# Two attention blocks: k and q by a seven-product scheme applied twice, partial sums moved between PSUM banks

## The chip, the cores and the metric

The kernel runs on one core of a Trainium2 chip. The metric is the device time of one execution, in microseconds (us). A core has TensorE (PE, matmul; PEld is its weight load), VectorE (DVE), ScalarE (ACT), GpSimd (POOL) and a sync engine (SP) whose queue issues the DMAs. Each engine works through its own instructions in the order in which the program lists them, and waits on semaphores for the others. Matmul results land in PSUM, which has eight banks of 512 fp32 columns on each of 128 partitions.

## The reference

Two attention blocks follow each other, each with its own weights; the second has the same form under other names. The input has 8 images of 512 channels and 32x32 = 1024 positions, all in fp32.

```python
xn = group_norm(x, 8 groups) * gamma + beta
qkv = einsum('oc,bchw->bohw', qkv_w, xn) + qkv_b          # 512 -> 3 * 512
q, k, v = split into 8 heads of 64
attn = softmax(einsum('bhds,bhdt->bhst', q, k) * 64 ** -0.5)
out = einsum('bhst,bhdt->bhds', attn, v)
x = x + einsum('oc,bchw->bohw', proj_w, out) + proj_b
```

## The kernel before

There are 16 jobs, one for each image and layer: images 0 and 1 in layer 0, then both in layer 1, then images 2 and 3, and so on. A job `n` has four 512x512 by 512x1024 products (k, q, v and the output projection, here K, Q, V, O) and the attention.

**The four products.** Each is cut into 2x2 blocks, and a scheme with seven block products in place of eight is applied once. The block of the weights goes through seven factors (`A11, A12, A22, S1..S4`; four of them are sums that VectorE makes once, in `factor`), and the other operand through sums in `tx` (for `xn`) or `to` (for the attention's output), made by `combine`. `product` issues one of the seven for one half `i` of the rows: two matmuls of 128x128 by 512 columns (L277), or for V four of 256 columns (L270). In the trace each fp32 matmul appears as two MATMUL records with a weight load each. `seven` runs the seven products for one `i`, in the order 1, 2, 6, 5, 7, 3, 4. It holds four PSUM banks `z, y, u, v`. Products 1, 6 and 7 add up in bank z, and after each of them `note` copies the partial sum out to SBUF before the next product adds to it; `join` adds what lies in SBUF to a bank and writes the result.

**The order of a job.** The loop over `n` is, for neighbouring jobs: attention of `n`, then K of `n+1`, O of `n`, V of `n+1`, Q of `n+1`, then attention of `n+1`. In Q's second half, `first_scores` puts the first two steps of the attention between the products.

**The attention.** It has 64 steps (four head pairs, two halves of the queries, eight key blocks of 128). A step is `scores` (four matmul groups on 64x64 quadrants, L470, into two PSUM banks `sc`), ScalarE's exp into a tile of `epool` (L475), VectorE's running sum `acc` (L479, L481), and `values` two steps later (L495). `epool` has four tiles; a tile is free once all its readers are done. `finish` closes each group of eight steps.

**What sets the order.** TensorE, ScalarE and VectorE keep the order of the program text. A small planner spreads side work: `later(delay, fn)` lists a function for a time on the planner's own clock, and `advance(us)`, called after each product and step, moves that clock and runs what is due. `chores` are side work tied to a step of the attention: the statistics (`reads`) and the normalisation (`steps`) of the next job. Tiles with the same tag share buffers: a tile's first write waits for the last reader of the one before. DMAs go out on SP's queue in order. `fetch` loads one whole weight matrix with all seven factors (1792 KB) into `wpool`, where each of K, V, Q, O has one buffer; on first use it loads the four raw blocks, and the finished factors are kept in DRAM (`keep`).

## Time and profile before

| What | Value |
|---|---|
| median of 4 runs | 3362.03 us (3360.58 to 3362.49) |
| the profiled execution | 3360.58 us; its span 3358.8 us |
| instructions | 50799 |
| TensorE busy | 3327.2 us (99% of the span) |
| VectorE busy | 2320.0 us (69%) |
| ScalarE busy | 1379.9 us (41%) |
| chain that ended last, by line | L470 27%, L495 25%, the products of L277 and L270 45% |
| granted TensorE clock | 0.999 |

How to read it: the span is one execution under the hardware profiler. The chain that ended last is followed back from the last instruction, at each step to what released it. A row of a group gives line, engine, operation, output<-inputs, shapes and count; behind the bar the busy time and the mean duration in ns of one; behind the second bar the engine's idle time just before these instructions and what ended it. In a timeline row the first number is the start and the second the duration. Matmuls are pipelined and their ends are modelled, so that neighbouring MATMUL rows overlap; the distance of their starts is what counts.

### The profile page before, as it was taken

How to read it: one execution, taken by the hardware profiler on the slowest of the kernel's cores; microseconds unless marked ns; L12 is line 12 of the kernel's file. 1: busy time of each engine (PE TensorE's matmuls, PEld its weight loads, DVE VectorE, ACT ScalarE, POOL GpSimd, SP SyncE). 2: the span in 40 equal slices, each digit the busy share in tenths (PEclk: the TensorE clock that was granted, in tenths of full speed). 3: DMA queues.
4: the chain of work that ended last, by engine and by line, in shares of the span. 5: the costliest groups of instructions: out<-in, count | busy, mean ns of one | idle time of the engine just before them, and what ended most of it. 6: DMA issues, size and time to landing. Idle time of an engine off the chain costs nothing.

```text
span 3358.8 us, 50799 instructions
## 1 busy us (share of the span) xinstructions
PE 3327.2 (99%) x20996; PEld 1481.8 (44%) x20996; DVE 2320.0 (69%) x3192; ACT 1379.9 (41%) x1535; POOL 16.9 (1%) x26
## 2 busy tenths in 40 slices
PE   7999999999999999999999999999999999999999
PEld 4335353453534535344353443535435354353533
DVE  4775957759487584865839668486684966848566
ACT  1543615336163361633516245162451624526153
POOL 0000000000000000000000000000000000000000
PEclk9999999999999999999999999999999999999999
DMA  5011010120201100021010010002102001000101
GB/s 194 12 51 51 22 60 15 53 81 22 76 15 36 48 24 23 15 74 63 22 72 18 33 52 21 23 18 83 52 21 73 18 33 52 21 22 22 45 11 44
DMA packets 79535, 141.82 MB, mean 42 GB/s; under 512 B 37568, under 2 KB 45760, under 8 KB 75200
## 3 DMA queue, kind: packets, MB, share of 16 engines
q1 hardware_dynamic: 79296, 138.50, 11.9%
q8 instruction: 166, 2.72, 0.3%
q14 instruction: 73, 0.60, 0.1%
HBM read 104.35 MB, written 31.98 MB: 41 GB/s over the span
## 4 chain that ended last, share of the span: by engine, by line
PE 98%; ACT 1%; DVE 0%; issue 0%; DMA 0%; POOL 0%; SPq 0%; DVEq 0%; POOLq 0%
PE sc L470 27%; PE po L495 25%; PE z L277 15%; PE u L277 10%; PE z L270 5%; PE y L277 5%; PE v L277 5%; PE u L270 3%; PE y L270 2%; PE v L270 2%; ACT e L475 1%; PE pp L440 1%; DVE stats L189 0%; DMA x<-x_dram 0%; ACT xn L225 0%
## 5 line engine op out<-in xcount | busy, mean ns | idle before, releaser
L475 ACT ACTIVATE e<-sc 128x1024 f32<-128x1024 f32 x1024 | 1047.0, 1024 | 645.4 <-PE sc L470 564.7
L470 PE MATMUL sc<-q,k 64*64 64x512 f32 x8192 | 1063.4, 591 | 6.6 <-ACT e L475 6.6
L495 PE MATMUL po<-e,v 64*64 64x512 f32 x8192 | 1057.3, 589 | 0.0
L481 DVE TENSOR_TENSOR acc<-acc,e 128x1024 f32<-128x1024 f32 x768 | 937.4, 1221 | 101.2 <-ACT e L475 52.9
L495 PEld LDWEIGHTS po<-e,v 64*64 64x64 f32 x8192 | 313.3, 133 | 565.6 <-issue 556.5
L470 PEld LDWEIGHTS sc<-q,k 64*64 64x64 f32 x8192 | 307.1, 133 | 565.1 <-issue 543.5
L326 ACT ACTIVATE sa<-z,vec_sb 128x512 f32<-128x512 f32 x128 | 88.0, 688 | 446.1 <-PE z L277 440.3
L277 PE MATMUL z<-xn,w 128*128 128x512 f32 x512 | 244.0, 599 | 3.6 <-ACT xn L225 3.6
L479 DVE TENSOR_TENSOR acc<-e,e 128x1024 f32<-128x1024 f32 x128 | 156.5, 1222 | 116.8 <-ACT e L475 115.5
L406 ACT ACTIVATE sb<-z,vec_sb 128x512 f32<-128x512 f32 x30 | 20.6, 688 | 340.9 <-PE z L277 340.9
L507 DVE TRANSPOSE_TENSOR_REDUCE r<-acc 128x32 f32<-128x1024 f32 x128 | 158.6, 1239 | 0.6
L378 ACT COPY sb<-u 128x512 f32<-128x512 f32 x32 | 18.8, 586 | 337.5 <-PE u L270 337.5
L277 PEld LDWEIGHTS z<-xn,w 128*128 128x128 f32 x512 | 96.4, 191 | 124.5 <-issue 119.1
L277 PE MATMUL z<-t,w 128*128 128x512 f32 x256 | 121.9, 599 | 4.7 <-DVE w L155 4.7
L277 PE MATMUL u<-xn,w 128*128 128x512 f32 x256 | 122.0, 599 | 0.0
L270 PE MATMUL z<-w,xn 128*128 128x256 f32 x512 | 121.0, 379 | 0.0
L277 PE MATMUL u<-t,w 128*128 128x512 f32 x256 | 120.5, 593 | 0.0
L277 PE MATMUL y<-xn,w 128*128 128x512 f32 x256 | 120.3, 592 | 0.0
L277 PE MATMUL v<-t,w 128*128 128x512 f32 x256 | 120.3, 592 | 0.0
L330 DVE TENSOR_TENSOR q<-sb 128x512 f32<-128x512 f32 x32 | 22.2, 693 | 137.9 <-ACT sb L326 137.9
L537 DVE TENSOR_TENSOR q<-q,rb 128x512 f32<-128x512 f32 x128 | 86.6, 677 | 40.4 <-DMA rb<-rd 40.4
L277 PE MATMUL z<-q,w 128*128 128x512 f32 x240 | 112.8, 592 | 0.0
(106 smaller groups left out, 2695.7 us busy)
## 6 DMA issues: line engine op xcount, KB each, us to landing
w<-keep SPq DMA_DIRECT2D x24, 1792.0 KB, 7.2
rb<-rd SPq DMA_DIRECT2D x256, 128.0 KB, 2.9
x<-x_dram SPq DMA_DIRECT2D x32, 512.0 KB, 5.5
out_dram<-x SPq DMA_DIRECT2D x64, 256.0 KB, 2.0
keep<-w SPq DMA_DIRECT2D x8, 1792.0 KB, 5.7
lr<-r SPq DMA_DIRECT2D x512, 4.0 KB, 1.7
w<-wqkv_dram SPq DMA_DIRECT2D x24, 256.0 KB, 5.1
w<-wp_dram SPq DMA_DIRECT2D x8, 256.0 KB, 6.1
```

The lines of the kernel that those rows point to most:

```text
L270: nc.tensor.matmul(ps[:, ti * CH : (ti + 1) * CH], block[:, cc, t0 : t0 + P], w[:, slot, cc, :], start=(first and ti == 0 and cc == 0), st ...
L277: nc.tensor.matmul(ps, w[:, slot, cc, i * P : (i + 1) * P], block[:, cc, :], start=(first and cc == 0), stop=(cc == 1), skip_group_check=True,
L326: nc.scalar.activation(out, ps, AF.Identity, bias=env.vec(layer, bias, oc))
L330: nc.vector.tensor_add(dst[:, 2 * oh + i, cols], a, b)
L440: nc.tensor.matmul(ps, w[:, cc, oc * P : (oc + 1) * P], qt[0][:, cc, cols], start=(cc == 0), stop=(cc == NC - 1),)
L470: nc.tensor.matmul(sc[h * HD : (h + 1) * HD, j, :], k[r, hp, k0 : k0 + HD], q[r, hp, sh * HALF : (sh + 1) * HALF], start=True, stop=True,)
L475: nc.scalar.activation(e, sc, AF.Exp, scale=SCALE)
L479: nc.vector.tensor_add(acc[g], es[i - 1], e)
L481: nc.vector.tensor_add(acc[g], acc[g], e)
L495: nc.tensor.matmul(po[g][j * HD : (j + 1) * HD, h, :], v[r, kc, d0 : d0 + HD], e[r, j, :], start=(kc == 0), stop=(kc == NT - 1),)
L507: nc.vector.tensor_reduce(r, a.rearrange("p j (b e) -> p (j b) e", e=RP), AX.X, ALU.add, apply_transpose=True,)
L537: nc.vector.tensor_mul(q[:, hp, cols], q[:, hp, cols], rb)
```

## The change

K and Q use the scheme twice: each of the seven outer block products is itself cut into 2x2 blocks, so that 49 products of 128x128 by 256 columns replace 28 matmuls of 512 columns. `deep_phases` builds 14 chains (seven outer products for K, seven for Q). A chain runs the seven inner products with four banks. Chains alternate on the two halves of PSUM and overlap: chain c's inner product j has slot 7c + 2j, so that in the steady state neighbouring slots belong to two chains. The result of an outer product (a tile of `epool`) is added into its quarter of k or q by `end`, on VectorE. The inner sums of the moving operand are made by `deep_sums` in the stages before.

In all four products a partial sum no longer goes to SBUF: in `chain`, ScalarE copies bank z to y after product 1 and to u after product 6, and the next product adds onto the copy. The bias of v moves into the output bias, made once per layer by `make_out_bias` with 16 one-column matmuls. `bias` in `deep_phases` gives outer products 2, 3, 4 and 5 a bias, and 1, 6 and 7 none. At the start eight matmuls write all banks once.

Weights stream through `ring`, eight tiles that hold one factor each (V, O) or the seven inner factors of one outer factor (K, Q). The inner factors are made in `prepare` at first use and kept in DRAM. The first layer's factors of V, K and Q are made at the start, the others as chores of the attentions of jobs 0 to 2 (`first_factors`). The order of a job becomes: attention of `n`, V of `n+1`, O of `n`, K and Q of `n+1`. The `to` sums take the tag k instead of v. `load_blocks` and `store_factors` are the DMAs of the former `fetch`, taken apart. V and O interleave their two halves.

The diff, cut to its core (the functions that it removes are printed above):

```diff
+FACTOR = {1: A11, 2: A12, 3: S4, 4: A22, 5: S1, 6: S2, 7: S3}
+ORDER = (1, 5, 6, 2, 7, 3, 4)
+OUTER = (1, 2, 6, 5, 7, 3, 4)
+QT = HALF // 2
+RING = 8
...
-    wpool = ctx.enter_context(tc.tile_pool(name="wpool", bufs=1))
+    ring = ctx.enter_context(tc.tile_pool(name="ring", bufs=RING))
...
+    plan, held, raw = deque(), {}, set()
+    def fetch():
+        if not plan:
+            return
+        key = plan.popleft()
+        n, which, o = key
+        layer = jobs[n][1]
+        w = ring.tile([P, NW, P], F32, tag="w", name=f"w_{which}_{n}_{o}")
+        held[key] = w
+        src = factors[which, layer][:, FACTOR[o]]
+        if which in (V, O):
+            nc.sync.dma_start(wide(w), src)
+        elif (which, layer, o) in deep:
+            nc.sync.dma_start(w, deep[which, layer, o])
+        else:
+            for at, i, j in ((A11, 0, 0), (A12, 0, 1), (A22, 1, 1), (S3, 1, 0)):
+                nc.sync.dma_start(w[:, at], src[:, j, i * P : (i + 1) * P])
+            raw.add(key)
+    def prepare(key):
+        if key not in raw:
+            return
+        raw.discard(key)
+        n, which, o = key
+        w = held[key]
+        for part in range(4):
+            factor(w, part)
+        keep = wdram.tile([P, NW, P], F32, name=f"deep_{which}_{jobs[n][1]}_{o}")
+        deep[which, jobs[n][1], o] = keep
+        later(1.0, lambda: nc.sync.dma_start(keep, w))
+    def used(key):
+        del held[key]
+        later(2.5, fetch)
...
+    def chain(product, put5, put, z, y, u, w):
+        def step(o):
+            product(o, {1: z, 5: w, 6: z, 2: y, 7: z, 3: u, 4: z}[o], o in (1, 5))
+            if o == 1:
+                nc.scalar.copy(y, z)
+            elif o == 5:
+                put5(w)
+            elif o == 6:
+                nc.scalar.copy(u, z)
+            elif o == 2:
+                put(0, 0, y)
+            elif o == 7:
+                put(1, 1, z)
+            elif o == 3:
+                put(0, 1, u)
+            else:
+                put(1, 0, z)
+        return step
+    def half_phase(n, which, src, t, group, order):
+        steps = []
+        for i in range(2):
+            z, y, u, w = (bank(i, b, f"{b}_{which}_{n}_{i}") for b in "zyuv")
+            steps.append(chain(*group(i), z, y, u, w))
+        thunks = []
+        for o in order:
+            key = (n, which, o)
+            thunks.append(lambda o=o: (steps[0](o), advance(1.72)))
+            def second(o=o, key=key):
+                steps[1](o)
+                if key in held:
+                    used(key)
+                advance(1.72)
+            thunks.append(second)
+        return thunks
...
+            def put(oh, sh, ps):
+                t0 = sh * NT // 2 + 2 * i
+                to_ = dst[:, t0 : t0 + 2, oh * CH : (oh + 1) * CH]
+                if sh == 0:
+                    nc.scalar.copy(to_, tokens(ps))
+                else:
+                    nc.vector.tensor_add(to_, tokens(ps), tokens(s5))
...
+            def put5(ps):
+                for oh in range(2):
+                    nc.vector.tensor_add(s5[:, oh, :], ps, at(oh, 1))
+            def put(oh, sh, ps):
+                oc = 2 * oh + i
+                more = s5[:, oh, :] if sh == 1 else at(oh, 0)
+                nc.vector.scalar_tensor_tensor(
+                    at(oh, sh), ps, out_bias[:, layer, oc : oc + 1], more, ALU.add, ALU.add
 +                )
...
+        chains = [(K, o) for o in OUTER] + [(Q, o) for o in OUTER]
+        tiles = {}
+        def begin(c):
+            which, o = chains[c]
+            if o == OUTER[0]:
+                name = "k" if which == K else "q"
+                dst[which] = acts.tile([P, NC, S], F32, tag=name, name=f"{name}_{n}")
+            if c + 2 < len(chains):
+                prepare((n,) + chains[c + 2])
+            e = epool.tile([P, 2, HALF], F32, tag="e", name=f"p_{n}_{c}")
+            tiles[which, o] = e
...
+            half = c % 2
+            z, y, u, w = (
+                bank(half, b, f"{b}d_{n}_{c}")[:, :QT] for b in ("vyuz", "zyuv")[(c // 2) % 2]
+            )
...
+            def put(oo, ph, ps):
+                to_ = e[:, oo, ph * QT : (ph + 1) * QT]
+                b = bias(oo)
+                if ph == 0:
+                    if b is None:
+                        nc.scalar.copy(to_, ps)
+                    else:
+                        nc.scalar.activation(to_, ps, AF.Identity, bias=b)
+                elif b is None:
+                    nc.vector.tensor_add(to_, ps, s5)
+                else:
+                    nc.vector.scalar_tensor_tensor(to_, ps, b, s5, ALU.add, ALU.add)
+            return chain(product, lambda ps: nc.scalar.copy(s5, ps), put, z, y, u, w)
+        def end(c):
+            which, o = chains[c]
+            used((n, which, o))
+            d = dst[which]
+            def quarter(oh, sh):
+                return d[:, 2 * oh : 2 * oh + 2, sh * HALF : (sh + 1) * HALF]
+            def p(k):
+                return tiles[which, k]
+            if o == 2:
+                nc.vector.tensor_add(quarter(0, 0), p(1), p(2))
+            elif o == 6:
+                nc.vector.tensor_add(p(6), p(6), p(1))
+            elif o == 5:
+                nc.vector.tensor_add(quarter(0, 1), p(6), p(5))
+            elif o == 7:
+                nc.vector.tensor_add(p(7), p(7), p(6))
+                nc.vector.tensor_add(quarter(1, 1), p(7), p(5))
+            elif o == 3:
+                nc.vector.tensor_add(quarter(0, 1), quarter(0, 1), p(3))
+            elif o == 4:
+                nc.vector.tensor_add(quarter(1, 0), p(7), p(4))
+        live = {}
+        def thunk(c, j):
+            def go():
+                if j == 0:
+                    live[c] = begin(c)
+                live[c](ORDER[j])
+                if j == 6:
+                    end(c)
+                advance(0.43)
+            return go
+        at = sorted((7 * c + 2 * j, c, j) for c in range(len(chains)) for j in range(7))
+        return [thunk(c, j) for _, c, j in at]
...
+            to[0] = acts.tile([P, 3, 2, HALF], F32, tag="k", name=f"to_{n}")
             combine(src, to[0], 0)
...
+    def deep_sums(n, direct_at, other_at):
+        def start():
+            d = acts.tile([P, 4, 7, QT], F32, tag="deep", name=f"deep_{n}")
+            deep_x[0], deep_t[0] = d[:, :, :4, :], d[:, :, 4:, :]
+        later(direct_at - 0.1, start)
+        for part in range(4):
+            later(direct_at + 1.7 * part, lambda part=part: inner_sums(part, True))
+            later(other_at + 1.7 * part, lambda part=part: inner_sums(part, False))
...
+    def first_blocks(w, layer, which, delay):
+        for part in range(4):
+            later(delay + 1.7 * part, lambda part=part: factor(w, part))
+        later(delay + 6.0, lambda: store_factors(w, layer, which))
+    def make_out_bias(w, layer):
+        pb = two_banks("sc", f"pb_{layer}")
+        for oc in range(NC):
+            for cc in range(NC):
...
+                nc.tensor.matmul(
+                    pb[:, 0, oc : oc + 1], w[:, at, cc % 2, o0 : o0 + P],
+                    env.vec(layer, BV, cc), start=(cc == 0), stop=(cc == NC - 1),
+                )
...
+    first = v_phase(0, (1, 2, 6, 5, 7, 3, 4), v0)
+    for thunk in first[:4]:
+        thunk()
+    for step in (
+        t[0], t[1], lambda: factor(v0, 0), lambda: factor(v0, 1), t[2], lambda: factor(v0, 2),
+        lambda: factor(v0, 3), t[3],
+    ):
+        step()
+    store_factors(v0, 0, V)
+    first_blocks(k0, 0, K, 0.1)
+    deep_sums(0, 7.0, 14.0)
+    def second_blocks():
+        q0 = acts.tile([P, NW, 2, CH], F32, tag="k", name="raw_q0")
+        load_blocks(q0, 0, Q)
+        first_blocks(q0, 0, Q, 6.0)
+    def first_plan():
+        plan.extend((0, K, o) for o in OUTER)
+        for _ in range(len(OUTER)):
+            fetch()
+    def second_plan():
+        plan.extend((0, Q, o) for o in OUTER)
+        fetch()
+    later(7.5, first_plan)
+    later(9.0, second_blocks)
+    for thunk in first[4:-1]:
+        thunk()
+    advance(0.0)
+    rest = first[-1:]
+    for n in range(-1, len(jobs)):
...
+                if n == 0:
+                    first_factors(more, [(O, 0), (V, 1)])
+                elif n == 1:
+                    first_factors(more, [(K, 1), (Q, 1)])
+                elif n == 2:
+                    first_factors(more, [(O, 1)])
...
+                chores[61] = lambda: (extend_plan(n + 1), [fetch() for _ in range(RING)])
...
+            out_sums(n, qt[0])
+            deep_sums(n + 1, 4.0, 27.0)
+            for thunk in v_phase(n + 1, ORDER):
+                thunk()
+            proj = proj_phase(n)
+            for thunk in proj[:-1]:
+                thunk()
+            rest = proj[-1:]
+        both = deep_phases(n + 1)
+        prepare((n + 1, K, OUTER[0]))
+        prepare((n + 1, K, OUTER[1]))
+        both[0]()
+        rest[0]()
+        if n >= 0 and jobs[n][1] == 1 and jobs[n][0] + 2 < B:
+            load_x(jobs[n][0] + 2)
         reads = steps = []
+        if n + 2 < len(jobs):
             reads, steps = norm_steps(n + 2)
+            if jobs[n + 2][1] == 1:
+                for i, step in enumerate(reads):
+                    later(9.0 + 6.0 * i, step)
+                reads = []
+        for i, thunk in enumerate(both[1:-3]):
+            if n < 0 and i == 14:
+                second_plan()
+            thunk()
+        att_n = n + 1
+        banks(0, "two")
+        att = Attention(att_n)
+        att.scores(0)
+        both[-3]()
+        att.scores(1)
+        both[-2]()
+        both[-1]()
+        banks(1, "two")
```

## The prediction

> **What bounds the kernel now.** The page comes first: busy shares, then the chain that ended last.

> ```profile
> PE 3327.2 (99%) x20996; PEld 1481.8 (44%) x20996; DVE 2320.0 (69%) x3192; ACT 1379.9 (41%) x1535; POOL 16.9 (1%) x26
> PE 98%; ACT 1%; DVE 0%; issue 0%; DMA 0%; POOL 0%; SPq 0%; DVEq 0%; POOLq 0%
> ```

> TensorE ends every stage, so a product removed there is time removed, as long as nothing new makes TensorE wait. Next the windows, for two stages of one job: K with O and V with Q are alike, here V, then the attention.

> ```profile
> 256.80:281.00 24.20, 24.20 (x113) 21.30 (x113) 9.69 (x15) 1.17 (x2) 0.00 (x0) 1.00 0.00 1
> 305.20:416.40 111.20, 110.76 (x1022) 39.49 (x1020) 95.81 (x126) 70.54 (x73) 1.01 (x1) 1.00 0.09 26
> ```

> The columns are length, then busy time of PE, PEld, DVE, ACT. VectorE has room in a projection stage and little in the attention. Third the timeline, for the price of a product and of handing over.

> ```profile
> 28.96 0.69 DVE L155 TENSOR_TENSOR w<-w 128x512 f32<-128x512 f32 x1
> 29.77 0.30 PEld L277 LDWEIGHTS z<-t,w 128*128 128x128 f32 x2 [5.46 <-issue]
> 38.44 1.88 PE L277 MATMUL v<-t,w 128*128 128x512 f32 x4
> ...
> 40.15 1.88 PE L277 MATMUL z<-t,w 128*128 128x512 f32 x4
> 40.35 0.69 DVE L330 TENSOR_TENSOR k<-v,sb 128x512 f32<-128x512 f32 x1 [0.82 <-PE v L277]
> ...
> 47.02 1.88 PE L277 MATMUL v<-t,w 128*128 128x512 f32 x4
> ...
> 55.64 1.89 PE L270 MATMUL z<-w,xn 128*128 128x256 f32 x8
> ...
> 62.55 1.89 PE L270 MATMUL y<-w,xn 128*128 128x256 f32 x8
> ```

> Five products of 512 columns lie between 38.44 and 47.02: 1.716 us each. Four of 256 columns, twice as many matmuls, lie between 55.64 and 62.55: 1.728. A reader starts 0.20 after the next product starts (40.15, 40.35); TensorE restarts 0.12 after VectorE ends (29.65, 29.77). Fourth the groups by shape:

> ```profile
> L326 ACT ACTIVATE sa<-z,vec_sb 128x512 f32<-128x512 f32 x128 | 88.0, 688 | 446.1 <-PE z L277 440.3 <-DVE k L330 4.5 <-DVE acc L481 1.3
> L323 ACT COPY sb<-u 128x512 f32<-128x512 f32 x64 | 37.5, 586 | 67.4 <-PE u L277 58.8 <-DVE q L330 7.5 <-DVE w L159 1.1
> L248 DVE TENSOR_TENSOR t<-xn 128x1024 f32<-128x1024 f32 x16 | 19.5, 1219 | 0.0
> L153 DVE TENSOR_TENSOR w<-w 128x512 f32<-128x512 f32 x8 | 5.5, 684 | 1.7 <-DMA w<-wqkv_dram 1.7
> L270 PEld LDWEIGHTS u<-w,t 128*128 128x128 f32 x256 | 48.6, 190 | 6.6
> ```

> **Columns.** K and Q are now 28 products of 1.716 = 48.05 a job; then 98 products of a quarter of 1.728, 0.432 = 42.34. Saved: 5.7 a job. [...]

> **The loop of a chain.** Two chains alternate on TensorE, one product each. Call them A and B, B seven products behind. Product 4 of B adds onto bank z, so VectorE's put after B's product 7 must have read z before. Ahead of this put in VectorE's queue stands end, the quarter add of A, and that waits for ScalarE's copy-out after A's product 4. So from A's product 4 to B's, seven products or 3.02 us later, this must fit:
> - the product 0.43 and the handover 0.20;
> - the copy-out 0.47 (688 for 512 columns, less 256 at 0.83 ns, the slope between the 512 columns of L323 and the 1024 of L475, 1024 ns), and 0.03 to VectorE;
> - the add 1.14 (1.22, less the 0.08 by which neighbours overlap: 29.57 starts before 29.65 in the timeline);
> - the put 0.48 (L408's 751 less 256 at VectorE's 1.04 ns) and 0.12 back to TensorE.

> That is 2.87, and 3.06 with a weight load of 0.19 that can't run ahead of the wait. It just closes, since both long forms (with bias) meet only once in seven. I take no loss; the bounds are 0 and 0.3 a chain. After outer product 7, end makes two adds, the second dependent on the first: 1.25 more with no room for it. TensorE's queue is in order, so I take 1.2 of waiting, once in K and once in Q: +2.4 a job, bounds 2.0 and 2.7. The other new waits are short. Product 6 needs ScalarE's copy from z to y: it has three products, 1.29 us, for 0.20 + 0.37 + 0.06 + 0.19. In V and O a slot is 1.72 us, so the same waits have four times the room; their VectorE work falls (V makes 4 puts for 14 notes and joins). [...]

> **Entry to attention.** Step 2's exp needs a tile of epool. Of its four tiles two hold exps 0 and 1, and two hold outer products 7 and 4 until the last end. Count from the end of the last product: exp 1 ends at 0.36 (it follows scores 1, two products earlier), then VectorE works off the first acc add, a put and the last end: 0.36 + 1.22 + 0.43 + 1.14 = 3.15. Exp 2 runs from 3.2 to 4.2 instead of from 1.15. Scores 4 need its bank; scores 2 and 3 and values 0 and 1 before them last 4 x 0.86 + 0.1 = 3.5. So scores 4 start at 4.3: +0.8 a job, bounds 0 and 1.2.

> **Other steps in steady state.** bn_stats for a layer-1 job (two of 0.67 and one of 0.21) come inside K and Q, in eight jobs, four each; the loop leaves VectorE 1.0 free per 3.02, so each overhangs 0.3: +9 in all, bounds 0 and 16. Inner sums (8 adds) lie in V and O, whose VectorE time falls. Jobs 0 and 2 prepare weights: four adds of 128x128 at 0.28 (684 less 384 columns), 1.0 ahead of a put with 0.15 spare: 0.85 for some eight chains, +7 for job 2, bounds 4 and 10. make_out_bias: 16 matmuls of one column, 32 weight loads at 0.19, plus restart: 7, twice, +14, bounds 8 and 22. Ring fetches are eight tiles ahead; one issue of about 0.5 on SP per 3 us; behind them queue only the sums' small DMAs: nothing. The factor adds in attention 0 to 2 (5 us in 111) fit.

> **The start.** Its DMA prices:

> ```profile
> 232.78 1.95 SPq L147 DMA_DIRECT2D w<-wqkv_dram  x4
> ...
> keep<-w SPq DMA_DIRECT2D x8, 1792.0 KB, 5.7
> w<-wqkv_dram SPq DMA_DIRECT2D x24, 256.0 KB, 5.1
> ```

> Four V products end at 25.0, as K's do now; the 4.7 us gap behind them closes, since VectorE makes no joins before the sums. V ends at 25.0 + 10 x 1.73 = 42.3. VectorE, with no joins to wait for, has V's factors at 24.5 and K's four at 28.5. Both are stored, 5.7 each: K's lie in DRAM about 36. first_plan then puts 28 small loads (seven tiles of four blocks) on SP, which wait for that store: 28 at 0.49 (1.95 for four) end at 50. Q's four blocks are queued behind them: issued to 52, landed at 57. By the planner's clock their factors come 16 us after V's fourth product, which is at the end of V, so they stand in VectorE's queue ahead of the put of the first chain. VectorE waits to 57 and works 4 us off (two factors of 0.68, two inner sums of 0.9, one preparation of 1.0). TensorE comes to product 4 of that chain nine products after V, at 46, and goes on at 61. K's first quarter add also waits for Q's blocks to be stored (same tag k): +3.5. Restart at half clock +1.6, preparation +7, double adds +2.4, 89 products 38.4, two scores 1.7: scores 2 at 115.6, against 99.1 in the trace: +17, bounds 6 and 26.

> **Sum.** 15 jobs x (-5.7+2.4) = -50; entry 16x0.8 = +13; statistics +9; job 2 +7; out_bias +14; start +17: **+10**. The profiled execution took 3360.6 with a span of 3358.8, 1.4 under the median 3362.0; on the median this is 3372. The half widths (start 10, out_bias 7, statistics 8, entry 8, double adds 5, preparation 3) combine to about 18: its own range is 3354 to 3390.

> **Rivals.** (1) The double adds are absorbed: a wait shifts later work, so the loop could regain it, and VectorE has 1 us free a turn. Against it: the products behind the waiting one are held in order. It decides where 0.9 of each 1.2 is regained in the 30 waits (-27: 3345, faster by 0.5%); with all of it -36: 3336. With the entry free too, 3323. (2) The loop doesn't close: copy from bank to bank, which no row shows, or the weight load costs 0.3 more than 3.02 allows, in each chain: 224x0.3 = +67, 3439; it decides from 0.05 a chain (+11). (3) The products are bound by weight loads: two of 0.190 in 0.432 leave 0.05; if waits keep loads from running ahead, 98x0.05x16 = +78, 3450.

> **How the numbers follow.** Forecast 0.48, rival 1 0.27, rival 2 0.18, rival 3 0.07. Within 0.2% (6.7 us), about what a measurement can tell from no change: the forecast gives 0.09 faster, 0.21 same, 0.70 slower; rival 1 gives 0.85, 0.10, 0.05; the others are slower. Sum: faster 0.27, same 0.13, slower 0.60. The range, 3334 to 3415, holds the forecast, most of rival 1 and the weaker half of rival 2.

> **What would show it.** TensorE waiting on VectorE's put once per K and once per Q, about 1.2 us; eight products of 256 columns still 3.46 us; scores of job 0 beginning about 17 us later, behind a VectorE wait for Q's blocks; scores 4 of each job waiting for exp. If TensorE shows waits at every chain, rival 2 is right; if K and Q last 42.4 us, rival 1; a job under 203 us from attention to attention (207.9 now; the forecast makes it 205.4) would break the forecast.

## The result, and the profile after

The changed kernel took 3366.2 us (median of 40 runs, 3361.9 to 3370.0) where the kernel before took 3361.9 (60 runs): ratio 1.0013, interval 1.0008 to 1.0017. It is slower by 4.3 us. The prediction was 3372, with 3334 to 3415 as its range and "slower" as its likeliest case.

The profiled execution has a span of 3363.0, 4.2 above that of before, and took 3364.9. The page's busy shares and its chain that ended last, after:

```profile
PE 3283.5 (98%) x22420; PEld 1740.9 (52%) x22420; DVE 2602.9 (77%) x3630; ACT 1727.4 (51%) x2557; POOL 17.5 (1%) x30
PE 90%; DVE 6%; ACT 2%; DMA 1%; issue 1%; SPq 0%; POOL 0%; DVEq 0%; ACTq 0%
```

TensorE is busy 43.7 us less and the span is longer all the same: TensorE's share of the chain went from 98% to 90%, and VectorE's from 0 to 6%. One job's attention and then the four projections behind it, as two windows (length, then busy time of PE, PEld, DVE, ACT):

```profile
953.86:1064.05 110.19, 109.16 (x1017) 38.67 (x1016) 101.92 (x138) 70.92 (x75) 1.01 (x1) 1.00 0.07 19
1064.05:1160.55 96.50, 94.47 (x385) 68.92 (x381) 63.66 (x93) 37.09 (x86) 0.00 (x0) 1.00 0.36 108
```

TensorE, which had next to no gap before, now stands idle about 1 us in the attention and 2 in the projections. The view of waits, TensorE's own, says for whom (total, times, longest):

```profile
PE vd L486 <- DVE p L502: 30.7, 32, 2.2
PE sc L593 <- ACT e L598: 16.0, 46, 0.6
PE vd L486 <- DVE p L500: 15.1, 5, 12.7
```

The first line is 32 waits for a put, two a job; the second is the entry to attention; the third is mostly one wait of 12.7, at the start.

The timeline of one double add (start, length; TensorE, ScalarE and VectorE lines about it, others left out):

```profile
1129.91 1.03 PE L486 MATMUL vd<-deep,w 128*128 128x256 f32 x4
...
1130.16 1.17 DVE L524 TENSOR_TENSOR p<-p,p 128x1024 f32<-128x1024 f32 x1
...
1131.37 1.23 DVE L525 TENSOR_TENSOR k<-p,p 128x1024 f32<-128x1024 f32 x1
...
1132.51 0.48 DVE L502 SCALAR_TENSOR_TENSOR p<-vd,bias_step,s 128x256 f32<-128x256 f32 x1
...
1133.05 0.70 PE L486 MATMUL vd<-deep,w 128*128 128x256 f32 x2 [1.25 <-DVE p L502]
```

Both adds of `end` (L524, L525) run ahead of the next chain's put (L502), and product 4 of that chain waits 1.25 for it. (K and Q of this job also read statistics for the next one; a reading ends at 1130.25, just ahead of the adds.) The last line lasts 0.70, against 0.59 elsewhere: its weight load starts with it at 1133.05, where that of the row behind, at 1133.58, starts 0.21 ahead. Counted from start to start of the products, TensorE loses 1.51 here and 1.05 in a job without statistics.

The timeline of the entry to attention, at the start of the period whose end holds these adds:

```profile
955.72 1.23 DVE L529 TENSOR_TENSOR q<-p,p 128x1024 f32<-128x1024 f32 x1
956.48 1.04 PE L618 MATMUL po<-e,v 64*64 64x512 f32 x8
957.03 1.94 ACT L598 ACTIVATE e<-sc 128x1024 f32<-128x1024 f32 x2 [2.60 <-DVE q L529]
...
958.11 1.09 PE L593 MATMUL sc<-q,k 64*64 64x512 f32 x8 [0.59 <-ACT e L598]
```

Exp 2 waits 2.60 for the last quarter add (L529) to free a tile, and scores 4 wait 0.59 for that exp. The other 30 waits of that line, 0.2 each at steps 25 and 33, are in the kernel before as well.

### The profile page after: what moved, and what is told of

It reads as the page before. It is cut to its first block, busy times and chain, and to the rows that moved or that the text cites. A ratio compares the mean times of both kernels' runs of the same rounds, so it can differ in the third digit from the quotient of the medians.

```text
span 3363.0 us, 56688 instructions
## 1 busy us (share of the span) xinstructions
PE 3283.5 (98%) x22420; PEld 1740.9 (52%) x22420; DVE 2602.9 (77%) x3630; ACT 1727.4 (51%) x2557; POOL 17.5 (1%) x30
## 3 DMA queue, kind: packets, MB, share of 16 engines
q1 hardware_dynamic: 154176, 259.12, 24.3%
## 4 chain that ended last, share of the span: by engine, by line
PE 90%; DVE 6%; ACT 2%; DMA 1%; issue 1%; SPq 0%; POOL 0%; DVEq 0%; ACTq 0%
PE sc L593 26%; PE po L618 25%; PE vd L486 6%; PE z L384 6%; PE z L419 6%; PE zd L486 6%; PE yd L486 2%; PE ud L486 2%; ACT e L598 2%; PE u L384 2%; PE v L384 2%; PE y L384 2%; PE u L419 2%; PE y L419 2%; PE v L419 2%; DVE p L524 1%
## 5 line engine op out<-in xcount | busy, mean ns | idle before, releaser
L486 PE MATMUL vd<-deep,w 128*128 128x256 f32 x960 | 278.5, 388 | 45.8 <-DVE p L502 30.7
L486 PE MATMUL zd<-deep,w 128*128 128x256 f32 x832 | 235.9, 383 | 5.4 <-DVE p L502 2.8
L486 PEld LDWEIGHTS vd<-deep,w 128*128 128x128 f32 x960 | 178.6, 191 | 98.5 <-DVE p L502 43.5
L486 PEld LDWEIGHTS zd<-deep,w 128*128 128x128 f32 x832 | 156.6, 191 | 41.7 <-DVE p L502 7.5
L335 ACT COPY yd<-vd 128x256 f32<-128x256 f32 x128 | 45.7, 357 | 185.5 <-PE vd L486 178.2
L426 DVE TENSOR_TENSOR s5o<-v,x 128x512 f32<-128x512 f32 x60 | 38.6, 684 | 101.9 <-PE v L419 101.9
L419 PE MATMUL z<-to,w 128*128 128x512 f32 x240 | 110.3, 592 | 0.0
L384 PE MATMUL z<-w,t 128*128 128x256 f32 x480 | 108.5, 379 | 0.0
L384 PEld LDWEIGHTS z<-w,xn 128*128 128x128 f32 x480 | 90.0, 190 | 23.8 <-issue 12.2
L384 PEld LDWEIGHTS z<-w,t 128*128 128x128 f32 x480 | 91.2, 190 | 12.4
## 6 DMA issues: line engine op xcount, KB each, us to landing
w<-keep SPq DMA_DIRECT2D x210, 256.0 KB, 2.7
out_dram<-x SPq DMA_DIRECT2D x64, 256.0 KB, 3.4
keep<-raw SPq DMA_DIRECT2D x5, 1792.0 KB, 5.8
```

Source lines behind the costliest of these rows:

```text
L335: nc.scalar.copy(y, z)
L384: nc.tensor.matmul(ps[:, ti * CH : (ti + 1) * CH], r[:, cc, t0 : t0 + P], w[:, cc, :], start=(start and ti == 0 and cc == 0), stop=(cc == ...
L419: nc.tensor.matmul(ps, w[:, cc, i * P : (i + 1) * P], r[:, cc, :], start=(start and cc == 0), stop=(cc == 1), skip_group_check=True,)
L426: nc.vector.tensor_add(s5[:, oh, :], ps, at(oh, 1))
L486: nc.tensor.matmul(ps, lhs[:, FACTOR[i], :], moving[i], start=start, stop=True, skip_group_check=True,)
```

## Where the time went, step by step

In the trace, one number carries each job: the time from its scores 2 to the next job's scores 2. Before it is 207.89 in fourteen of the fifteen periods and 208.00 in one. After, the twelve periods from job 3 on take 205.41 (six, without statistics) and 206.6 (six, with). Each period holds the attention and O of one job and V, K and Q of the next, so each term of the prediction's sum has a place of its own:

| stretch | prediction, us against before | measured |
|---|---|---|
| start, to scores 2 of job 0 | +17 (115.6) | +13.5 (112.6) |
| job 0 to 1: out_bias, statistics | +5.6 | +2.6 |
| job 1 to 2: preparation, statistics | +5.6 | +6.6 |
| job 2 to 3: out_bias | +4.5 | +3.0 |
| six periods without statistics | 6 x -2.5 | 6 x -2.48 |
| six with statistics | 6 x -1.4 | 6 x -1.27 |
| last attention | +0.8 | +1.1 |
| sum | +10 | +4.2 |

The steady state was forecast to 0.1 us a job. The difference of 6 us lies in the start and the three early periods (7.0 below the forecast, against 1.2 above it in the rest), and the runs below say why.

## Experiments

Every ratio is to the kernel before, run on the same chip (its median there lay between 3361.7 and 3362.6); "the changed kernel" is the 3366.2 above. Periods and starts are read from one profiled execution a run; "attention 0 begins" stands for the start of scores 2 of job 0 in it.

**1. The second add later.** After outer product 7, `end` writes its quarter in one add and leaves the other for a later thunk:

```diff
-                nc.vector.tensor_add(p(7), p(7), p(6))
-                nc.vector.tensor_add(quarter(1, 1), p(7), p(5))
+                nc.vector.tensor_add(quarter(1, 1), p(7), quarter(0, 1))
+                held_back.append(lambda: nc.vector.tensor_add(p(7), p(7), p(6)))
...
+                if j == 5 and held_back:
+                    held_back.pop()()
```

> After outer product 7, end makes one add (quarter(1,1) = p(7) + quarter(0,1)); the second, p(7) += p(6), is issued behind the two puts of the next chain. The sum and the number of adds stay the same. Theory (VectorE's queue order: two dependent adds of 1.22 us stand ahead of the next chain's put): the two waits of 1.05 us per job at product 4 vanish, at most 0.1 comes back at the next chain, a plain job falls from 205.4 to about 203.4 us, the total from 3366 to about 3336. Rival (TensorE waits there for ScalarE's copies from bank to bank and its copy-out): the waits stay, 3366.

Measured 3332.3, ratio 0.9913 (0.9899 to 0.9926). TensorE's waits for this put, where the view had 30.7 us in 32 waits:

```profile
PE vd L486 <- DVE p L502: 1.4, 2, 0.9
```

A period without statistics fell from 205.41 to 203.36, by 2.05: the two losses of 1.05, so the loop had regained nothing of them. One addition in the wrong place of a queue had cost 1% of the kernel.

**2. A fifth tile for the entry.**

```diff
-    epool = ctx.enter_context(tc.tile_pool(name="epool", bufs=LEAD + 2))
+    epool = ctx.enter_context(tc.tile_pool(name="epool", bufs=LEAD + 3))
```

> epool has five tiles instead of four. Theory (exp 2 of each attention waits for a tile that the last quarter add frees): exp 2 starts about 2 us sooner, TensorE's wait at scores 4 (0.6 us, with the weight load behind it 0.8) goes in all 16 jobs: -13, 3353. Rival (the entry is held by ScalarE's order: exp 0, exp 1 and the copy-out ahead of exp 2): no change, 3366.

Measured 3352.1, ratio 0.9971 (0.9962 to 0.9981). The wait of scores for exp:

```profile
PE sc L593 <- ACT e L598: 6.6, 30, 0.2
```

It was 16.0 in 46, longest 0.6. The period fell by 0.82 in every job, so the entry's cause is the tile and its price the forecast 0.8.

**3. Q's blocks first.** Q's raw blocks are loaded before K's 28 small loads instead of after:

```diff
+    later(7.4, second_blocks)
     later(7.5, first_plan)
-    later(9.0, second_blocks)
```

> At the start second_blocks (Q's four raw blocks) is put on SP's queue ahead of first_plan (28 small loads for K). Theory (VectorE is held by the factoring of Q's blocks, whose loads are queued behind the 28): TensorE's wait of 12.7 us at the first product 4 falls under 2 us, and with it the restart at half clock (1.9); but Q's factors are now stored behind the 28 loads, so the first quarter add of K, which shares the tag k with Q's blocks, waits 4 to 6 us: attention of job 0 starts at about 104 instead of 112.6, total about 3358. Rival (VectorE is simply late with preparation and inner sums): the start moves by under 2 us, 3365.

Measured 3363.8, ratio 1.0007 (0.9998 to 1.0016). The profiled attention begins at 107.1 instead of 112.6, but the profiled execution, 3358.3, is the fastest of eleven, and the median fell by 2.4 only, against other runs on another chip: between the two expectations, and too small to tell them apart by time. The trace says more. The single TensorE wait of 12.67 became two of 4.0; SP's queue and VectorE, start of this kernel:

```profile
35.70 0.98 SPq L144 DMA_DIRECT2D raw_q<-wqkv_dram  x2
36.72 13.74 SPq L181 DMA_DIRECT2D w<-keep  x28
50.56 2.67 SPq L194 DMA_DIRECT2D deep<-w  x4
53.32 1.16 SPq L159 DMA_DIRECT2D keep<-raw_q  x1
```

```profile
61.20 1.23 DVE L518 TENSOR_TENSOR k<-p,p 128x1024 f32<-128x1024 f32 x1 [4.76 <-DMA keep<-raw_q]
```

Q's blocks come early, but their store (tag k) is issued only at 53.3, behind the 28 loads, and K's first quarter add waits for it. The queue's order sets the start, as the prediction had it; changing it once moves the wait to the next transfer.

**4. The copies from bank to bank, twice.** Each `nc.scalar.copy` from z to y and to u in K and Q runs two times:

```diff
-                nc.scalar.copy(y, z)
+                for _ in range(copies):
+                    nc.scalar.copy(y, z)
```

> In K and Q each of ScalarE's copies from bank z to y and from z to u is made twice, 28 copies more per job at 0.27 us from start to start. Theory (these copies have about 0.4 us to spare before products 6 and 7, ScalarE has 1 us free per seven products): 0.2 to 0.5 us per job from copy-outs that come later, +3 to +8, about 3371. Rival (the copies are on the path of every chain): 0.27 twice per chain, 14 chains, 16 jobs: +60 to +120, 3426 or more.

Measured 3378.7, ratio 1.0050 (1.0036 to 1.0064): 12.5 more, above the theory's 3 to 8 and far below the rival's 60. A period without statistics grew by 0.9. TensorE's starts in such a job show where: 0.24 at the first chain's product 7, 0.17 more at each double add, and 0.06 or 0.07 at product 4 of five chains that had no wait. The first of these five, in the changed kernel and here:

```profile
914.97 1.23 DVE L518 TENSOR_TENSOR k<-p,p 128x1024 f32<-128x1024 f32 x1 [0.88 <-ACT p L498]
916.42 1.03 PE L486 MATMUL zd<-deep,w 128*128 128x256 f32 x4
```

```profile
921.71 1.22 DVE L520 TENSOR_TENSOR k<-p,p 128x1024 f32<-128x1024 f32 x1 [1.11 <-ACT p L500]
922.93 1.09 PE L488 MATMUL zd<-deep,w 128*128 128x256 f32 x4
```

The TensorE rows hold two products each; product 4 is the second, and it starts at 916.85 and 923.37. In the changed kernel the quarter add starts 1.88 before it; here, where the row shows the 0.06 of waiting, 1.66. So **the loop of a chain had 0.22 us to spare**: it closes, and one copy more opens it.

**5. Statistics in the attention.** The readings of a layer-1 job's statistics become chores of the attention before:

```diff
-            if jobs[n + 2][1] == 1:
-                for i, step in enumerate(reads):
-                    later(9.0 + 6.0 * i, step)
-                reads = []
```

> The statistics of a layer-1 job's input (two bn_stats of 0.67 us and one of 0.21, four times a job, eight jobs) are read during the attention of the job before instead of inside K and Q. Theory (each reading sits in VectorE's queue ahead of a put that has under 0.3 us to spare): the profile after shows 206.6 from attention to attention in jobs with statistics and 205.4 in those without; all twelve plain periods become 205.4, eight times 1.2 = 9 us less, 3357. Rival (the 1.2 belongs to something else in those jobs, or the attention, where VectorE is busy 101 of 111 us, can't take 1.55 us four times): periods stay at 206.6, 3366, or the attention grows by some 6 us in eight jobs, 3405.

Measured 3355.4, ratio 0.9980 (0.9971 to 0.9989). Of the twelve periods from job 3 on, eleven are 205.4 and one is 205.65. The statistics cost 1.2 a job in K and Q and nothing in the attention, where VectorE is busy 103 of 111 us (run 8's windows): at 93% it still had room for the 1.55 us, since nothing waits for it at once there.

**6. Preparation behind the puts.**

```diff
-            if c + 2 < len(chains):
-                prepare((n,) + chains[c + 2])
...
+                if j == 2 and c + 2 < len(chains):
+                    prepare((n,) + chains[c + 2])
```

> In jobs 0 and 2 the four adds that prepare a weight tile come two products later, behind the puts of the chain instead of ahead of its first one. Theory (four adds of 0.28 us ahead of a put with about 0.15 to spare cost 0.75 in each of some ten chains): job 2 loses 7.5 us (its K and Q stall 11.4 against 3.5 in other jobs with statistics), job 0 about 6, time 3353. Rival (VectorE has no room for the four adds anywhere in a chain of 3.02 us while it prepares): stalls move to a later put and the time stays at 3363 to 3366.

Measured 3359.3, ratio 0.9991 (0.9982 to 0.9999): 6.9 less, half of what was expected. K and Q of job 2 stall 7.3 instead of 11.4, not 3.5 (0.9 of the 11.4 is half clock, see below). The stalls that remain are at the chains with statistics, 1.2 where a job without preparation has 0.25: VectorE has room for the preparation or for the statistics, and not for both in one chain. Run 8 has the same job without statistics, and its period is 1.2 longer than a plain one.

**7. The start, with fewer loads ahead.** Run 3's order, and four tiles of K asked for at once, three later:

```diff
-        for _ in range(len(OUTER)):
+        for _ in range(4):
             fetch()
+        for _ in range(3):
+            later(12.8, fetch)
```

> Q's raw blocks are asked for ahead of K's factor tiles, as in the run with Q's blocks first, and three of the seven tiles of K are asked for 5 us later. Theory (SP's queue is what the start waits for: in the run with Q's blocks first the store of Q's blocks was issued at 53.3 us, behind 28 loads and 4 small ones, and VectorE's first quarter add waited 4.76 us and TensorE twice 4.0): the store goes out some 6 us sooner, one of the two 4.0 us waits goes, attention 0 begins at 103 to 105 instead of 107.1; time 1 to 3 us under that run, 3361. Rival (the waits are set by the landing of Q's blocks themselves or by VectorE's factors, not by the order of the queue): attention 0 at 107 and 3364.

Measured 3362.7, ratio 1.0003 (0.9994 to 1.0012). The time is near the theory's, its reason isn't: attention 0 begins at 110.9, later than in run 3. The store went out at 53.9, no sooner, because VectorE got to Q's last factor at 53.2; and the tiles asked for late came late:

```profile
60.87 0.29 DVE L149 TENSOR_TENSOR w<-w 128x128 f32<-128x128 f32 x1 [6.65 <-DMA w<-keep]
```

This theory fell: behind the queue, VectorE's own order sets the store.

**8. All five edits** (1, 2, 5, 6 and the start of 7).

> All edits together: the second add held back, a fifth tile for the entry, statistics in the attention, preparation behind the puts, the start in the new order. Theory (each removes a stall of its own on TensorE): 3366 less 34, 14, 9, 13 and 5 = 3291, 2.1% under the kernel before; from attention to attention about 201.4. Rival (the stalls cover one another, so that VectorE's next late put takes the place of each): no better than the second add and the fifth tile, 3318.

Measured **3293.7**, ratio 0.9796 (0.9783 to 0.9809), 2.0% under the kernel before. The chain and TensorE's three longest waits:

```profile
PE 96%; DVE 2%; ACT 1%; DMA 1%; issue 0%; SPq 0%; POOL 0%; DVEq 0%
```

```profile
PE sc L596 <- ACT e L601: 6.6, 30, 0.2
PE z L384 <- ACT xn L259: 3.6, 1, 3.6
PE vd L484 <- DVE p L498: 2.3, 1, 2.3
```

From attention to attention it takes 202.5 in eleven of the twelve periods from job 3 on (202.8 in one): 5.35 less than before. The 5.7 of K and Q's fewer columns arrives nearly whole. The stalls were separate ones, and their savings add up: runs 1, 2, 5, 6 and 7 alone saved 33.9, 14.1, 10.8, 6.9 and 3.5, 69 in all, and together they save 72.5.

**9 and 10. Two other starts for it**: all seven tiles at once (as in 3), and five at once with two 3 us later.

> All five edits together, but with the start of the run with Q's blocks first: all seven tiles of K asked for at once behind Q's blocks. Theory (asking late for three tiles cost more than it gave, as the run of the start alone showed: VectorE waited 6.65 us for a tile there): attention 0 begins 2 to 4 us before the 98.5 of the run with all edits, time 3290 to 3292. Rival (the store of Q's blocks, then issued behind 28 loads, is late again, with 4 us of waiting twice): attention 0 at 102, 3297.

> All five edits together; behind Q's blocks five of K's seven tiles are asked for at once and two 3 us later, a middle way. If the length of the row ahead of the store of Q's blocks and the lateness of the last tiles both count, this is better than either: attention 0 at 95 to 98, 3289 to 3292. If only one counts, it lies between the other two starts.

Measured 3295.9 and 3295.9, ratios 0.9799 (0.9785 to 0.9812) and 0.9801 (0.9788 to 0.9814): not to be told from run 8. Attention 0 begins at 102.6 and 101.5, against 98.5; by the last attention the three profiles lie within 2.5 us (3150.6, 3152.9 and 3150.5 in runs 8 to 10). By time neither start is better. What evens them out is the next finding: the period from job 0 to job 1 is 208.05, 209.66 and 206.50 in runs 8 to 10, and the one from job 2 to job 3 is 209.66, 206.36 and 208.05, with the same work.

**11. The bias matmuls three times over.** In `make_out_bias`:

```diff
-        for oc in range(NC):
+        for oc in 3 * list(range(NC)):
```

> make_out_bias, called in attention 0 and in attention 2, runs its 16 one-column matmuls three times over instead of once (same result, 64 weight loads more in each). Theory (the profile after: 32 loads in 3.73 us, 0.114 from start to start, and nothing else on TensorE meanwhile): 7.3 us more in each of the two attentions, 14.6 in all, 3381. Rival (the term of the prediction, 0.19 a load, the duration in its row): 12.2 each, 24.3 in all, 3390.

Measured 3392.8, ratio 1.0090 (1.0075 to 1.0106): 26.6 more. The total is near the rival's, but neither theory held. Loads started 0.112 apart (a little under the 0.114 of the expectations) until the granted clock fell. Four windows of attention 0 (the last three columns are the granted clock, the DMA share and GB/s):

```profile
137.00:141.00 4.00, 4.00 (x38) 3.71 (x34) 3.62 (x8) 0.59 (x1) 0.00 (x0) 1.00 0.05 12
141.00:153.00 12.00, 12.00 (x62) 12.00 (x61) 0.00 (x0) 0.00 (x0) 0.00 (x0) 0.53 0.06 20
153.00:158.50 5.50, 5.50 (x29) 2.39 (x33) 1.69 (x3) 1.02 (x1) 0.00 (x0) 0.50 0.00 0
159.00:161.00 2.00, 2.00 (x24) 0.63 (x20) 0.61 (x2) 1.15 (x2) 0.00 (x0) 1.00 0.00 0
```

After 40 loads the clock is at half, the rest start 0.213 apart, and the scores behind them run at half for 5 us more. The changed kernel itself has it, on a small scale, in attention 2:

```profile
564.53 1.98 PE L593 MATMUL sc<-q,k 64*64 64x512 f32 x8
566.30 1.81 PE L618 MATMUL po<-e,v 64*64 64x512 f32 x8
567.94 1.03 PE L593 MATMUL sc<-q,k 64*64 64x512 f32 x8
```

Eight matmuls that take 1.04 take 1.98 and 1.81 there, right behind the 32 loads: 1.7 us. In attention 0 of the same execution the clock stayed at 1.00. The same 32 loads stand in two attentions of the changed kernel and of runs 1 to 10, which makes 22 cases. In five the clock stayed at 1.00. In eleven it was at half for 3.41 us. In six it was at half for 6.83 us, and fell so early that the loads themselves took 4.3 to 4.7 us from the first start to the last instead of 3.5 to 3.7.

```profile
132.26:135.67 3.41, 1.98 (x18) 1.98 (x18) 0.00 (x0) 1.00 0.01 1
135.67:139.09 3.42, 1.75 (x16) 1.67 (x15) 0.16 (x1) 1.00 0.28 81
139.09:142.50 3.41, 0.00 (x0) 0.00 (x0) 0.00 (x0) 1.00 0.00 0
552.10:555.51 3.41, 2.22 (x20) 2.22 (x20) 0.00 (x0) 1.00 0.03 6
555.51:558.93 3.42, 2.77 (x14) 2.68 (x13) 0.16 (x1) 0.50 0.23 77
```

In attention 0 the loads fill 1.98 and 1.75 us of two stretches, and the clock holds; in attention 2 they fill 2.22 of one, and the next runs at half. All 22 cases sort themselves so: where the loads filled 2.17 us or more of a stretch the clock fell at its end (17 cases), where they filled 2.05 or less of each it stayed (5). The grid lies differently in each execution (its first point, counted back, is 1.2 us after the span's start in the changed kernel, 2.6 in run 1 and 3.1 in run 4), so the same code falls on either side.

**12. The same, with 96 columns streamed instead of one.**

```diff
-                    pb[:, 0, oc : oc + 1], w[:, at, cc % 2, o0 : o0 + P],
-                    env.vec(layer, BV, cc), start=(cc == 0), stop=(cc == NC - 1),
+                    pb[:, 0, 96 * oc : 96 * oc + 96], w[:, at, cc % 2, o0 : o0 + P],
+                    env.vec_sb[:, v0 + cc : v0 + cc + 96], start=(cc == 0), stop=(cc == NC - 1),
```

> As the run with the bias matmuls three times over, but each of them streams 96 columns instead of one (the other 95 are neighbours and zeros, and are not used). In that run 40 loads went at 0.114 us, the granted clock then fell to 0.50, the remaining loads took 0.215, and the clock stayed at 0.50 for some 5 us of scores behind them: 26.6 us more than the changed kernel. Theory (what lets the clock fall is that hardly any columns stream, not that weights are loaded): the clock stays at 1.00, the loads at 0.114 cover the 96 columns (96/256 of 0.216 = 0.081 us), 96 of them take 11 us in each attention, 14.6 more than the changed kernel, 3381. Rival (a run of weight loads counts as idle whatever streams beside it): clock 0.50 again, 3393 or more.

Measured 3376.6, ratio 1.0043 (1.0029 to 1.0056): 16 us less than run 11, for 96 times the columns. Clock and loads in attention 0:

```profile
135.00:146.00 11.00, 11.00 (x104) 10.88 (x104) 3.37 (x7) 0.33 (x1) 0.00 (x0) 1.00 0.09 26
146.00:150.00 4.00, 4.00 (x40) 1.50 (x44) 2.03 (x4) 2.05 (x2) 0.00 (x0) 1.00 0.00 0
```

The clock stays at 1.00, 96 loads take 10.96 us and start 0.112 apart. The theory held; the total is 4 below its 3381, of which 1.7 is the half clock of attention 2, which went too.

## Why the prediction was right, and where it was off

**The columns** (-5.7 a job): right. Products of 256 columns start 0.432 apart in K and Q wherever nothing waits, and run 8, with the waits gone, is 5.35 a job under the kernel before.

**The double adds** (1.2 twice a job): right in place and number, 1.05 in size. The mechanism is shown by run 1: with one add out of the way, 33.9 us go. Rival 1, that the loop regains the waits, is out. What it said of the time with the adds absorbed, 3336, is what run 1 gives when they really are (3332).

**The loop of a chain** (it just closes, 2.87 to 3.06 in 3.02): right. Run 4 puts the room at 0.22, so 2.80 is needed; the weight load is not part of the loop as long as TensorE doesn't wait, since it then starts 0.21 ahead of its product. Rival 2 is out for this kernel, by 0.22 us.

**Weight loads that bind** (rival 3): out; the products keep their 0.432.

**The entry** (+0.8): right in cause and size, by run 2.

**Statistics** (0.3 at four chains of eight jobs, +9): 1.2 a job, 0.26 at three chains and 0.46 at a double add. Run 5 took 10.8 away. The place and the cause were right; the size was luck in part, since readings of 1.55 against 1.0 of free time overhang by 0.55, and the prediction gives no sum for its 0.3.

**Preparation** (+7 in job 2): 7.9 by the period from job 1 to job 2, 214.52. Of this 0.9 is the clock: TensorE waits 2.15 at a put there, is busy 1.25 of a stretch of 3.41 us, and the next 3.41 us run at half. In the profiles of runs 3, 11 and 12, where the clock held, the period is 213.64, which makes the forecast 7.0. Run 6, where it held too, takes off 3.3 while the statistics stand beside it.

**out_bias** (7 twice): the term that was mis-sized most. It took the 0.190 of the load's row for its pace. That is how long one load lasts; with nothing else to do, the next starts 0.112 after it, since they overlap:

```profile
135.90 3.73 PE L740 MATMUL pb<-vec_sb,raw 128*128 128x1 f32 x32
```

The whole call costs 3.8 in attention 0 and 5.5 in attention 2, where the halved clock is the difference: -4.7 of the 6 us by which the sum was too high. This execution was a lucky one: by the periods of the 22 cases a call costs 3.8 where the clock holds, 5.5 with one stretch at half and 7.1 with two. With the counts above that is about 11 for both calls on average, an estimate, against the forecast 14; a clock that falls under the loads was no part of the forecast. The prediction's own first rows had warned: it read starts, not lengths, for the products of 512 columns.

**The start** (+17): 13.5. The forecast's order held up to TensorE's restart: the last of Q's loads was issued at 52.1 (forecast 52), VectorE went on at 56.5 (forecast 57) and TensorE at 60.1 (forecast 61).

```profile
50.11 1.97 SPq L144 DMA_DIRECT2D raw_q<-wqkv_dram  x4
```

```profile
56.50 0.69 DVE L149 TENSOR_TENSOR raw_q<-raw_q 128x512 f32<-128x512 f32 x1 [8.80 <-DMA raw_q<-wqkv_dram]
60.11 1.22 PE L486 MATMUL vd<-deep,w 128*128 128x256 f32 x2 [12.67 <-DVE p L500]
67.43 1.23 DVE L518 TENSOR_TENSOR k<-p,p 128x1024 f32<-128x1024 f32 x1 [1.31 <-DMA keep<-raw_q]
```

By the times it was 3.0 us too long (115.6 against 112.6; the +17 is rounded up). Of this 0.9 lies there. Behind the restart two terms were wrong in opposite directions. K's first quarter add was priced at 3.5; VectorE waits 1.31 for the store, and TensorE loses about 0.1 by it (the first product 4 behind that add starts 0.77 late, and 0.67 late in job 2, which prepares weights too and has no such wait). The half clock was priced at 1.6 (in the kernel before it lasts 3.4 us at the restart, from 30.0); it lasts 6.0 us from the restart, to 66.1, and costs 3.05 in seven products. The preparation of job 0 comes to 6.4. That the total came out near is luck in part.

**The copies to PSUM.** No row of before shows ScalarE copy from bank to bank. The groups by shape, after, 512 and 256 columns from PSUM, for each size first to PSUM, then to SBUF:

```profile
L335 ACT COPY y<-z 128x512 f32<-128x512 f32 x62 | 35.3, 570 | 75.1 <-PE z L384 39.8 <-PE z L419 35.3
L401 ACT COPY s<-v 128x512 f32<-128x512 f32 x32 | 18.7, 586 | 36.8 <-PE v L384 36.8
L335 ACT COPY yd<-vd 128x256 f32<-128x256 f32 x128 | 45.7, 357 | 185.5 <-PE vd L486 178.2 <-ACT p L498 0.3
L504 ACT COPY s<-vd 128x256 f32<-128x256 f32 x96 | 35.7, 372 | 45.0 <-PE vd L486 45.0
```

To PSUM they take 570 and 357 ns, to SBUF 586 and 372: 15 ns or so less at both sizes, which decides nothing here.

**One reading of a row.** The prediction calls 0.83 ns the slope between L323 (586 for 512 columns) and L475 (1024 for 1024); by these rows it is 0.855. The copy-out is 0.47 by either, and L498 measures 0.473.

Open is which order of the start is best: three were tried with all other edits in, and the time doesn't tell them apart. With the half clock behind the loads taken out of the three profiles (5.0, 3.3 and 1.8 us in runs 8 to 10, from the two periods above), run 8's start would be some 3 to 4 us ahead; that is an estimate from one execution each.

## What to carry to other kernels

When an engine at 98% sheds work, look at what stands ahead of its next wait in the helper's queue: here one addition of 1.2 us that nobody needed yet took back a third of the gain, and moving it (with four such edits) made a loss of 0.1% a gain of 2%. Count the loop from a product to the one that waits for it in single instructions; a margin of 0.2 us decided. Price a burst of instructions by the distance of their starts (0.112 us for the loads here), not by the duration in a row (0.190), and a burst of weight loads also by the half clock that it can leave behind (1.6 to 1.7 us a stretch here).

## What the runs showed of the hardware

**The granted clock fell while TensorE worked.** In run 11 the array had no gap, 96 weight loads with one column each, and 4.4 us after the first load in attention 0 and 5.3 us in attention 2 the granted clock went to 0.50; in run 12 the same loads with 96 columns each kept it at 1.00. Both issue 96 loads with 96 matmuls there; what differs is the columns that stream. In the 22 shorter cases 2.17 us of one-column loads or more in one stretch of 3.41 went with a fall at its end, and 2.05 or less did not; one stretch at half cost 1.6 to 1.7 us of the attention behind it. At the start the clock fell while TensorE stood still: it stops at 47.4 us, and the clock is at 0.50 from 52.4 to 66.1.

**A weight load's pace went with the clock**: the loads of run 11 start 0.112 us apart at a granted clock of 1.00, and 0.213 at 0.50.
